# Attention layers of a graph network on one core: engines held to program order, row-half transposes, reciprocals through memory

## The chip, the core and the metric

The kernel runs on one core of a Trainium2 chip. The core has a matrix engine (TensorE, PE in the profile; its weight loads are the row PEld), a vector engine (VectorE, DVE), a scalar engine (ScalarE, ACT), a general one (GpSimd, POOL) and a queue for transfers (SyncE, SP). Each of them takes its own instructions one after the other, and semaphores tie the engines together. The matrix engine writes to PSUM, a memory of eight banks, from which DVE and ACT read. The metric is the device time of one execution in microseconds; less is better.

## The reference, cut to what matters

```python
# x: (32, 512, 64), adj: (512, 512); all float32
h = relu(layernorm(x)); x = x + graph_layer_0(h, adj)
h = relu(layernorm(x)); x = x + graph_layer_1(h, adj)

# layer 2: one attention head
h = relu(layernorm(x))
Wh = h @ W.T
e = leaky_relu((Wh @ a1)[:, :, None] + (Wh @ a2)[:, None, :], 0.2)
att = softmax(where(adj > 0, e, -9e15), axis=-1)
x = x + elu(att @ Wh)

# layer 3: eight heads of width 128, then one more attention over their outputs
h = relu(layernorm(x))
def gat_layer(x, W, b):
    g = x @ W
    s = einsum('bnd,bmd->bnm', g, g) * adj
    s = where(s == 0, -1e16, s)
    return softmax(s, axis=2) @ g + b
cat = leaky_relu(concat over the 8 heads of gat_layer(h, Wh[i], bh[i]), 0.01)
x = x + leaky_relu(gat_layer(cat, W_out, b_out), 0.01)
```

## The kernel before

Layers 0 and 1 come first and take the first 265 us or so; they are not touched. Layers 2 and 3 are one stream of *units*. A unit holds two attention matrices of 512 x 512: two graphs of the batch in layer 2 (`Gat`, 16 units), two heads of one graph in layer 3 (`Heads`, 128 units), or the last attention of two graphs (`Out`, 16 units). The order of units is written out: the 16 `Gat`, then the `Heads` of one graph after the other (four units each), with an `Out` put in after the third unit of the graph that follows its pair; so eight `Heads` and one `Out` repeat, and the last `Out` comes after three empty places.

A unit takes four steps in each of its phases, one for each block of 128 rows or columns (`C` = 4). The function `run` walks over steps `k` and lets the units that are in flight do one step of each phase. In step `r` of the unit whose scores are computed, the following happens:

- `scores(r)`: PE multiplies (L547, tile `s_ps`, two banks, two buffers). In `Gat` there is nothing to do here.
- `transpose(j)` of the unit before, with an offset of five steps (`C + LAG`): the exponentials `p_att` are turned, eight transposes of 128 x 128 into two banks `pt_ps` (L413), which ACT copies into `pt_att` (L418). With `j == 1`, `recips` follows: DVE takes the reciprocals of the row sums (L432), PE spreads them over partitions with 16 matmuls against the identity (L436, tile `rec_ps`), and ACT copies the result to `recb` (L444).
- `values(j)`, offset six: PE multiplies `pt_att` with the values into `av` (L425), one bank with one buffer.
- `end(step)`, offset ten: step 0 multiplies `av` by `recb` on DVE (`normalize`, L448); step 1 of `Heads` multiplies with the head's weights (L619, `y_ps`, two products) and lets ACT make `cat` of it (L624); step 2 of `Gat` and `Out` adds the result to `x` (`back`).
- `prep(step)` of the unit to come, four steps ahead: `Heads` normalizes its graph at step 0 when it is the graph's first unit (`hn`, `hx`), and makes `g` at step 2 (L591, copied by ACT at L599). `Out` multiplies `cat` with `W_out` into `gT_ps` (L642), four products in each of its four steps, then makes `gT` and `gV`.
- `soft(r)`: DVE multiplies the scores with the adjacency (L536), finds the zeros (L540), and adds and takes the row minimum for each of the two matrices (L397); ACT takes the exponentials and their sums (L401).

What a matmul of float32 is in the source stands as two in the profile; a transpose is one.

The pool `ps_m` has three banks under one tag. `pt_ps`, `rec_ps`, `y_ps`, `g_ps`, `gT_ps`, `hx_ps`, `back_ps` and the small products of `Gat` take turns in them. `ps_s` has the four banks of the scores, `ps_v` the one of `av`.

The order in which instructions stand on each engine is not that of the source: a planner of the tile framework sets it from dependencies, priorities and its own costs. In layer 3 it puts, on PE, a block of transposes, a block of values and a block of scores in turn, and fits the other products between them; on DVE it lets `normalize`, the reciprocals and the work on `hn` slip in between the four operations of a soft step.

Of the kernel before, what the change touches and what calls it, by code (L numbers as in the profile page):

```python
# [8 lines left out]
F32 = mybir.dt.float32  # L9
# [5 lines left out]
P = 128  # L15
# [7 lines left out]
def gnn_stack_kernel(  # L23
# [22 lines left out]
    nc = tc.nc  # L46
    B, N, F = x.shape
    C = N // P
    H, _, D = w_heads.shape
# [4 lines left out]
    const = ctx.enter_context(tc.tile_pool(name="const", bufs=1))  # L54
    xpool = ctx.enter_context(tc.tile_pool(name="xpool", bufs=1))
    tiny = ctx.enter_context(tc.tile_pool(name="tiny", bufs=4))

    ident = const.tile([P, P], F32, name="ident")
# [10 lines left out]
    for g in range(NG):  # L69
        xg = xpool.tile([P, G, C, F], F32, name=f"x{g}")  # L70
        step = 2 if g == 0 else G
# [37 lines left out]
    wo_sb = const.tile([P, H, F], F32, name="wo_sb")  # L109
# [224 lines left out]
        return wk.tile([P, N], F32, name=name, tag="row", bufs=2 * H + 6)  # L334

    wk = ctx.enter_context(tc.tile_pool(name="work_b", bufs=2))
    ps_s = ctx.enter_context(tc.tile_pool(name="ps_s", bufs=2, space=PSUM))
    ps_m = ctx.enter_context(tc.tile_pool(name="ps_m", bufs=3, space=PSUM))
    ps_v = ctx.enter_context(tc.tile_pool(name="ps_v", bufs=1, space=PSUM))
# [1 line left out]
    adj_f = adj_p.rearrange("p c k q -> p c (k q)")  # L341
    neg = const.tile([P, C, N], F32, name="neg")
    nc.vector.tensor_scalar(neg, adj_f, 0.0, GAT_NEG, op0=OP.is_le, op1=OP.mult)

# [30 lines left out]
    def halves(k):  # L377
        return slice(k * F, (k + 1) * F)

    class Pair:  # L380
# [26 lines left out]
        def transpose(self, j):  # L407
            pt = pbuf.tile([P, 2, N], F32, name="pt_att", bufs=3)
            self.pts = getattr(self, "pts", []) + [pt]
            for k in range(2):  # L410
                ps = ps_m.tile([P, N], F32, name="pt_ps", tag="m")
                for r in range(C):
                    nc.tensor.transpose(  # L413
                        ps[:, r * P : (r + 1) * P],
                        self.p[:, k, r, j * P : (j + 1) * P],
                        ident,
                    )
                nc.scalar.copy(pt[:, k, :], ps)  # L418

        def values(self, j):  # L420
            pt = self.pts.pop(0)
# [6 lines left out]
                )  # L428

        def recips(self):  # L430
            rec = tiny.tile([P, 2, C], F32, name="rec")
            nc.vector.reciprocal(rec, self.sum)  # L432
            ps = ps_m.tile([P, N], F32, name="rec_ps", tag="m")
            for r in range(C):
                for k in range(2):
                    nc.tensor.matmul(  # L436
                        ps[halves(k), r * P : (r + 1) * P],
                        lhsT=rec[:, k, r : r + 1].to_broadcast([P, F]),
                        rhs=ident,
                        start=True,  # L440
                        stop=True,
                    )
            self.recb = wk.tile([P, N], F32, name="recb")
            nc.scalar.copy(self.recb, ps)  # L444

        def normalize(self):
            self.o = wk.tile([P, N], F32, name="o_att")
# [107 lines left out]
    class Heads(Pair):  # L555
# [9 lines left out]
        def prep(self, step):  # L565
            b, i = self.b, self.i
            if step == 0 and i == 0:
# [9 lines left out]
                    h[:, :, 0, :], h[:, :, 0, :], 0.0,  # L577
                    rstd[:, cols, None].to_broadcast([P, C, F]), op0=OP.max, op1=OP.mult,
                )
                nc.vector.tensor_copy(h[:, :, 1, :], h[:, :, 0, :])  # L580
                Heads.hn[b] = h
                Heads.hx[b] = pair_transpose(
                    ps_m, lambda n: wk.tile([P, N], F32, name=n), h, "hx",
                    nc.vector.tensor_copy, "m",
                )
            elif step == 2:
                rows = halves(i % 2)
# [41 lines left out]
    class Out(Pair):  # L629


        def __init__(self, b):
            self.b = b

        def prep(self, step):
            b = self.b
            if step == 0:
                self.gps = ps_m.tile([P, N], F32, name="gT_ps", tag="m")
            if step < 4:
                for h in (2 * step, 2 * step + 1):  # L640
                    for k in range(2):
                        nc.tensor.matmul(  # L642
                            self.gps[halves(k), :], lhsT=wo_sb[:, h, :],
                            rhs=Heads.cat[b + k, h], start=(h == 0), stop=(h == H - 1),
                        )
            if step == 3:
                self.gT = wk.tile([P, N], F32, name="gT")
                nc.scalar.copy(self.gT, self.gps)
                ps = ps_m.tile([P, C, P], F32, name="gV_ps", tag="m")
                for c in range(C):  # L650
                    nc.tensor.transpose(ps[:, c], self.gT[:, c * P : (c + 1) * P], ident)
                self.gV = wk.tile([P, C, P], F32, name="gV")
                nc.scalar.copy(self.gV, ps)
# [30 lines left out]
    def run(units):  # L684
        units = units + [None] * 3

        def at(k, off):
            u, j = divmod(k - off, C)
            return (units[u], j) if 0 <= u < len(units) else (None, j)

        for j in range(C):
            units[0].prep(j)
        for k in range(len(units) * C):
            cur, r = at(k, 0)
            if cur:
                cur.scores(r)
            u, j = at(k, C + LAG)
            if u:
                u.transpose(j)
                if j == 1:  # L700
                    u.recips()
            u, j = at(k, C + LAG + 1)
            if u:
                u.values(j)
            u, j = at(k, 2 * C + LAG + 1)
            if u:
                u.end(j)
            u, j = at(k, -C)
            if u:
                u.prep(j)  # L710
            if cur:
                cur.soft(r)

    flow_stats = []
    order = [Gat(b) for b in range(0, B, 2)]
# [45 lines left out]
```

## Time and profile before

| | us |
|---|---|
| median of 3 runs | 2914.0 (2912.58 to 2915.0) |
| the profiled execution, its own time | 2918.14 |
| its span, first to last instruction | 2916.4 |
| PE busy | 2813.4 |
| PEld busy | 1380.0 |
| DVE busy | 2407.5 |
| ACT busy | 2049.0 |
| POOL busy | 52.7 |

The mean TensorE clock that was granted is 0.983 of the full one. The profile comes from one execution, and times of single instructions are taken from it. A row of the timeline gives the start and the length in us, the engine, the line, the operation, the output and input tiles and their sizes; in brackets stands how long the engine was idle before it, and which engine, tile and line ended that. Matmuls are pipelined and their ends are modelled, so the distance between starts tells what one costs.

### The profile page before, as it was taken

The page shows a single profiled execution, that of the slowest core. Times are in us where ns is not written, and L with a number is a line of the kernel's source. Part 1 is how long each engine was busy: PE and PEld are TensorE (multiplying, and loading weights), DVE is VectorE, ACT ScalarE, POOL GpSimd, SP SyncE. Part 2 cuts the span into 40 slices and gives each one's busy share as a digit, 9 for nine tenths or more (in the row PEclk, how much of TensorE's full clock was granted, in tenths as well). Part 3 has the DMA queues.
Part 4 walks back from the last instruction along what each step waited for, and adds up shares of the span by engine and source line. Part 5 has one row for each costly group of instructions (what it writes and reads, how often), then busy time and mean ns, then how long its engine had stood idle before and what let it go on. Part 6 is the DMA issues. An engine that isn't in the chain of part 4 may idle for free.

```text
span 2916.4 us, 41809 instructions
## 1 busy us (share of the span) xinstructions
PE 2813.4 (96%) x15532; PEld 1380.0 (47%) x15532; DVE 2407.5 (83%) x4870; ACT 2049.0 (70%) x4687; POOL 52.7 (2%) x49
## 2 busy tenths in 40 slices
PE   7998887899999999999999999999999999999998
PEld 4555544444444444444444444444444444444443
DVE  6665889899798988888888888888888888888884
ACT  2333767677777778777777777777777777777775
POOL 3000000000000000000000000000000000000000
PEclk9998999899999999999999999999999999999999
DMA  3000000000000000000000000000000000000000
GB/s 86 1 1 1 1 1 1 1 1 1 1 5 4 1 4 1 4 1 5 1 4 1 4 1 4 1 5 1 4 1 5 1 5 1 4 1 4 1 4 4
DMA packets 9916, 13.10 MB, mean 4 GB/s; under 512 B 1016, under 2 KB 9376, under 8 KB 9584
## 3 DMA queue, kind: packets, MB, share of 16 engines
q1 hardware_dynamic: 4752, 5.24, 0.5%
q10 hardware_dynamic: 4208, 4.19, 0.5%
q8 instruction: 122, 2.00, 0.3%
q0 software_dynamic: 752, 0.99, 0.2%
q14 instruction: 82, 0.67, 0.1%
HBM read 6.23 MB, written 4.19 MB: 4 GB/s over the span
## 4 chain that ended last, share of the span: by engine, by line
PE 88%; DVE 6%; ACT 3%; issue 1%; POOL 1%; DMA 1%; POOLq 0%; DVEq 0%; ACTq 0%
PE av L425 20%; PE pt_ps L413 20%; PE s_ps L547 19%; PE rec_ps L436 6%; PE g_ps L591 5%; PE y_ps L619 4%; PE nt_ps L240 4%; PE gT_ps L642 3%; PE nt1b_ps L240 2%; ACT p_att L401 1%; DVE s_att L536 1%; PE po L251 1%; DVE t_att L397 1%; PE wh_ps L474 1%; DVE l_att L397 1%
## 5 line engine op out<-in xcount | busy, mean ns | idle before, releaser
L401 ACT ACTIVATE p_att<-t_att,negmax 128x512 f32<-128x512 f32 x1152 | 825.3, 717 | 466.3 <-DVE negmax L397 466.2
L536 DVE TENSOR_TENSOR s_att<-s_ps,adj_p 128x1024 f32<-128x1024 f32 x576 | 703.3, 1221 | 228.6 <-PE s_ps L547 228.6
L413 PEld LDWEIGHTS pt_ps<-ident,p_att 128*128 128x128 f32 x5120 | 554.8, 142 | 492.6 <-ACT p_att L401 187.5
L418 ACT COPY pt_att<-pt_ps 128x512 f32<-128x512 f32 x1280 | 679.3, 581 | 120.7 <-PE pt_ps L413 120.5
L397 DVE CUSTOM_DVE_ANT_0 t_att<-s_att,t_att 128x512 f32<-128x512 f32 x1152 | 752.3, 687 | 13.4
L413 PE MATMUL pt_ps<-ident,p_att 128*128 128x128 f32 x5120 | 714.5, 282 | 12.6 <-ACT p_att L401 7.5
L547 PE MATMUL s_ps<-hx,g 64*128 64x512 f32 x2048 | 661.2, 625 | 2.0 <-DVE s_att L536 2.0
L425 PE MATMUL av<-pt_att,hn 128*64 128x512 f32 x2048 | 579.0, 611 | 0.0
L540 DVE TENSOR_SCALAR t_att<-s_att 128x1024 f32<-128x1024 f32 x576 | 393.1, 683 | 24.3 <-ACT pt_att L418 0.5
L547 PEld LDWEIGHTS s_ps<-hx,g 64*128 64x128 f32 x2048 | 204.8, 185 | 311.3 <-issue 121.3
L401 ACT ACTIVATION_READ_ACCUMULATOR p_att<-t_att,negmax 128x1 f32 x1152 | 216.0, 187 | 0.0
L436 PE MATMUL rec_ps<-ident,rec 128*64 128x128 f32 x2560 | 186.6, 284 | 16.9 <-DVE rec L432 10.6
L436 PEld LDWEIGHTS rec_ps<-ident,rec 128*64 128x64 f32 x2560 | 144.4, 139 | 50.6 <-issue 26.5
L624 ACT ACTIVATE cat<-y_ps,bh 128x512 f32<-128x512 f32 x256 | 159.6, 672 | 4.4 <-PE y_ps L619 4.4
L425 PEld LDWEIGHTS av<-pt_att,hn 128*64 128x64 f32 x2048 | 115.6, 135 | 76.5 <-issue 76.2
L619 PE MATMUL y_ps<-o_att,wh_sb 64*128 64x512 f32 x512 | 145.8, 641 | 1.6 <-ACT pt_att L418 0.8
L591 PE MATMUL g_ps<-hx,m 64*128 64x512 f32 x256 | 144.6, 645 | 1.0 <-ACT pt_att L418 0.9
L642 PE MATMUL gT_ps<-cat,wo_sb 128*64 128x512 f32 x512 | 131.4, 595 | 0.0
L448 DVE TENSOR_TENSOR o_att<-av,recb 128x512 f32<-128x512 f32 x160 | 108.9, 681 | 21.8 <-PE av L425 20.6
L240 PE MATMUL nt_ps<-adj_t,hn 128*128 128x512 f32 x256 | 116.5, 598 | 0.0
L397 DVE DVE_READ_ACCUMULATOR2_ANT negmax<- 128x1 f32 x1280 | 104.7, 82 | 0.0
L444 ACT COPY recb<-rec_ps 128x512 f32<-128x512 f32 x160 | 93.9, 587 | 8.8 <-PE rec_ps L436 8.8
(131 smaller groups left out, 1930.4 us busy)
## 6 DMA issues: line engine op xcount, KB each, us to landing
out_dram<-x SPq DMA_DIRECT2D x32, 128.0 KB, 1.8
x<-in_x_dram ACTq DMA_DIRECT2D x3, 1024.0 KB, 13.7
x<-in_x_dram ACTq DMA_DIRECT2D x4, 256.0 KB, 7.9
adj_raw<-in_adj_dram SPq DMA_DIRECT2D x1, 1024.0 KB, 5.3
wh_sb<-in_L_gnn_Wh_dram POOLq DMA_DIRECT2D x2, 256.0 KB, 8.0
wo_sb<-in_L_gnn_W_out_dram POOLq DMA_DIRECT2D x1, 256.0 KB, 7.9
wl<-in_L_gnn_net_params_dram POOLq DMA_DIRECT2D x4, 16.0 KB, 7.0
bias_b<-in_L_gnn_bias_dram POOLq DMA_DIRECT2D x1, 32.0 KB, 7.6
```

Source lines behind the costliest of these rows:

```text
L240: nc.tensor.matmul(p, lhsT=lhs(k), rhs=adj_t[:, k, :], start=(k == 0), stop=(k == C - 1))
L397: nc.vector.tensor_tensor_reduce(out=ns[k], in0=s[k], in1=t[k], scale=-1.0, scalar=BIG, op0=OP.add, op1=OP.min, accum_out=self.negmax[:, k ...
L401: nc.scalar.activation(self.p[:, k, r, :], ns[k], AF.Exp, bias=self.negmax[:, k, r : r + 1], scale=-1.0, accum_out=self.sum[:, k, r : r + 1],)
L413: nc.tensor.transpose(ps[:, r * P : (r + 1) * P], self.p[:, k, r, j * P : (j + 1) * P], ident,)
L418: nc.scalar.copy(pt[:, k, :], ps)
L425: nc.tensor.matmul(self.av[halves(k), :], lhsT=self.v(k, j), rhs=pt[:, k, :], start=(j == 0), stop=(j == C - 1),)
L436: nc.tensor.matmul(ps[halves(k), r * P : (r + 1) * P], lhsT=rec[:, k, r : r + 1].to_broadcast([P, F]), rhs=ident, start=True, stop=True,)
L536: nc.vector.tensor_tensor(s, ps, adj_f[:, r, None, :].to_broadcast([P, 2, N]), OP.mult)
L540: nc.vector.tensor_scalar(t, s, 0.0, FLOW_NEG, op0=OP.is_equal, op1=OP.mult)
L547: nc.tensor.matmul(u.s_ps[:, k], lhsT=g[halves(k), r * P : (r + 1) * P], rhs=x[halves(k), :], start=True, stop=True,)
L591: nc.tensor.matmul(ps, lhsT=m2[rows, 2 * i : 2 * i + 2, :].rearrange("p h f -> p (h f)"), rhs=self.x[rows, :], start=True, stop=True,)
L619: nc.tensor.matmul(ps, lhsT=wh_sb[halves(k), h, :], rhs=self.o[halves(k), :], start=True, stop=True,)
```

## The change

The part of `run` with all units is put under `tc.manual_schedule` for PE, DVE and ACT: on these three engines the instructions stand in the order in which the source emits them. The source order itself is changed: `end` now comes before `values`, `soft` comes before `recips` and `prep`, and `recips` moves from `j == 1` to `j == 0` of the transposes.

The transposes of a step are made on row halves: 16 of 64 x 128 in place of eight of 128 x 128, the halves of the rows in a bank each, and ACT copies each bank to interleaved places of `pt_att`.

The reciprocals no longer go through PE and ACT. DVE writes them into one of two zeroed tiles of 128 x 32, turns that tile in blocks of 32 x 32, SP writes the rows to a buffer in DRAM with four transfers, and two further transfers read them back, spread over 64 partitions each, into `recb`.

The product with `W_out` is spread: `Out.prep` is also called four and eight steps earlier, and puts one head's products in a step, from step -7 to step 1; `gT` is copied at step 1, `gV` made at step 2. Two copies of `Heads.prep` (for `hn` and `hx`) go from DVE to ACT.

```diff
+    dram = ctx.enter_context(
+        tc.tile_pool(name="dram", bufs=3, space=bass.MemoryType.DRAM)
+    )
...
+    recs = [const.tile([P, 32], F32, name=f"rec{i}") for i in range(2)]
+    for rec in recs:
+        nc.gpsimd.memset(rec, 0.0)
...
         def transpose(self, j):
             pt = pbuf.tile([P, 2, N], F32, name="pt_att", bufs=3)
             self.pts = getattr(self, "pts", []) + [pt]
+            ps = [ps_m.tile([P, 2, C, F], F32, name="pt_ps", tag="m") for half in range(2)]
             for k in range(2):
-                ps = ps_m.tile([P, N], F32, name="pt_ps", tag="m")
                 for r in range(C):
-                    nc.tensor.transpose(
-                        ps[:, r * P : (r + 1) * P],
-                        self.p[:, k, r, j * P : (j + 1) * P],
-                        ident,
-                    )
-                nc.scalar.copy(pt[:, k, :], ps)
+                    for half in range(2):
+                        nc.tensor.transpose(
+                            ps[half][:, k, r],
+                            self.p[halves(half), k, r, j * P : (j + 1) * P],
+                            ident[halves(half), halves(half)],
+                        )
+            pth = pt.rearrange("p k (r half q) -> p k r half q", r=C, half=2)
+            for half in range(2):
+                nc.scalar.copy(pth[:, :, :, half, :], ps[half])
...
         def recips(self):
-            rec = tiny.tile([P, 2, C], F32, name="rec")
-            nc.vector.reciprocal(rec, self.sum)
-            ps = ps_m.tile([P, N], F32, name="rec_ps", tag="m")
-            for r in range(C):
-                for k in range(2):
-                    nc.tensor.matmul(
-                        ps[halves(k), r * P : (r + 1) * P],
-                        lhsT=rec[:, k, r : r + 1].to_broadcast([P, F]),
-                        rhs=ident,
-                        start=True,
-                        stop=True,
-                    )
+            rec = recs[0]
+            recs.append(recs.pop(0))
+            nc.vector.reciprocal(rec[:, : 2 * C], self.sum.rearrange("p k r -> p (k r)"))
+            rect = tiny.tile([P, 32], F32, name="rect")
+            nc.vector.transpose(rect, rec)
+            row = dram.tile([2 * C, P], F32, name="rec_row")
+            for q in range(P // 32):
+                nc.sync.dma_start(
+                    row[:, q * 32 : (q + 1) * 32], rect[q * 32 : q * 32 + 2 * C, :]
+                )
             self.recb = wk.tile([P, N], F32, name="recb")
-            nc.scalar.copy(self.recb, ps)
+            for k in range(2):
+                nc.sync.dma_start(
+                    self.recb[halves(k), :],
+                    row[k * C : (k + 1) * C]
+                    .rearrange("(o r) p -> o (r p)", o=1)
+                    .to_broadcast([F, N]),
+                )
...
         # Heads.prep, step 0
-                nc.vector.tensor_copy(h[:, :, 1, :], h[:, :, 0, :])
+                nc.scalar.copy(h[:, :, 1, :], h[:, :, 0, :])
...
-                    nc.vector.tensor_copy, "m",
+                    nc.scalar.copy, "m",
...
         # Out.prep
-            if step == 0:
+            if step == -2 * C + 1:
                 self.gps = ps_m.tile([P, N], F32, name="gT_ps", tag="m")
-            if step < 4:
-                for h in (2 * step, 2 * step + 1):
-                    for k in range(2):
-                        nc.tensor.matmul(
-                            self.gps[halves(k), :], lhsT=wo_sb[:, h, :],
-                            rhs=Heads.cat[b + k, h], start=(h == 0), stop=(h == H - 1),
-                        )
-            if step == 3:
-                self.gT = wk.tile([P, N], F32, name="gT")
-                nc.scalar.copy(self.gT, self.gps)
+            h = H - 2 + step if step >= 0 else 2 * C - 1 + step
+            if 0 <= h < (H if step >= 0 else H - 2):
+                for k in range(2):
+                    nc.tensor.matmul(
+                        self.gps[halves(k), :], lhsT=wo_sb[:, h, :],
+                        rhs=Heads.cat[b + k, h], start=(h == 0), stop=(h == H - 1),
+                    )
+                if h == H - 1:
+                    self.gT = wk.tile([P, N], F32, name="gT")
+                    nc.scalar.copy(self.gT, self.gps)
+            if step == 2:
                 ps = ps_m.tile([P, C, P], F32, name="gV_ps", tag="m")
...
-        for k in range(len(units) * C):
+        with tc.manual_schedule(engines={PE, DVE, Activation}):
+            for j in range(C):
+                units[0].prep(j)
+            for k in range(len(units) * C):
                 cur, r = at(k, 0)
                 if cur:
                     cur.scores(r)
                 u, j = at(k, C + LAG)
                 if u:
                     u.transpose(j)
-                    if j == 1:
-                        u.recips()
+                u, j = at(k, 2 * C + LAG + 1)
+                if u:
+                    u.end(j)
                 u, j = at(k, C + LAG + 1)
                 if u:
                     u.values(j)
-                u, j = at(k, 2 * C + LAG + 1)
-                if u:
-                    u.end(j)
-                u, j = at(k, -C)
-                if u:
-                    u.prep(j)
                 if cur:
                     cur.soft(r)
+                u, j = at(k, C + LAG)
+                if u and j == 0:
+                    u.recips()
+                for early in range(2, -1, -1):
+                    u, j = at(k, -C * (early + 1))
+                    if u and (early == 0 or isinstance(u, Out)):
+                        u.prep(j - early * C)
```

The rows of the profile before name the lines of the kernel before. In the changed kernel the transposes stand at L422 and their copies at L429, values at L436, the reciprocal at L446, normalize at L465, scores at L564, the soft step at L553, L557, L404 and L408, g at L608, y at L636, W_out at L661.

## The prediction

> **What bounds the kernel now.** I read the page first, then stretches, then one stretch of the timeline, and last the waits. The page says that PE is busy nearly all the time and at full clock:
>
> ```profile
> PE 2813.4 (96%) x15532; PEld 1380.0 (47%) x15532; DVE 2407.5 (83%) x4870; ACT 2049.0 (70%) x4687; POOL 52.7 (2%) x49
> ...
> PE   7998887899999999999999999999999999999998
> PEclk9998999899999999999999999999999999999999
> ```
>
> The table of stretches for the layer-3 part (640 to 2800 us; columns: length, then busy time of PE, PEld, DVE, ACT, POOL, then clock) shows PE busy 2156.6 of 2160 us, DVE 1844.8:
>
> ```profile
> 640.00:2800.00 2160.00, 2156.58 (x12217) 1009.94 (x12217) 1844.83 (x3636) 1633.85 (x3775) 0.00 (x0) 1.00 0.01 3
> ```
>
> In it stand 2156 matmuls of L547, 16 to a unit (4 steps): 134.75 units, **16.03 us a unit**. In the list of waits for that stretch DVE waits for PE:
>
> ```profile
> DVE s_att L536 <- PE s_ps L547: 211.8, 257, 3.1
> ```
>
> One stretch of the timeline (start, length, both us) gives the spacings that I use:
>
> ```profile
> 1512.33 1.22 DVE L536 TENSOR_TENSOR s_att<-s_ps,adj_p 128x1024 f32<-128x1024 f32 x1
> ...
> 1513.58 0.69 DVE L540 TENSOR_SCALAR t_att<-s_att 128x1024 f32<-128x1024 f32 x1
> ...
> 1514.31 0.69 DVE L397 CUSTOM_DVE_ANT_0 t_att<-s_att,t_att 128x512 f32<-128x512 f32 x1
> ...
> 1514.93 0.69 DVE L397 CUSTOM_DVE_ANT_0 t_att<-s_att,t_att 128x512 f32<-128x512 f32 x1
> 1515.05 0.72 ACT L401 ACTIVATE p_att<-t_att,negmax 128x512 f32<-128x512 f32 x1 [0.25 <-DVE negmax L397]
> ...
> 1515.77 0.71 ACT L401 ACTIVATE p_att<-t_att,negmax 128x512 f32<-128x512 f32 x1
> ...
> 1515.95 1.09 PE L413 MATMUL pt_ps<-ident,p_att 128*128 128x128 f32 x8
> ...
> 1516.47 0.56 ACT L599 COPY g<-g_ps 128x512 f32<-128x512 f32 x1
> 1516.94 1.07 ACT L418 COPY pt_att<-pt_ps 128x512 f32<-128x512 f32 x2
> ...
> 1516.98 1.08 PE L425 MATMUL av<-pt_att,hn 128*64 128x512 f32 x4
> ...
> 1517.99 1.13 PE L547 MATMUL s_ps<-hx,g 64*128 64x512 f32 x4
> ```
>
> A PE step is three blocks, 1.03, 1.01 and about 1.05 us from start to start: some 0.86 of work and 0.17 lost at each change of array shape. A DVE step in program order is 1.25 + 0.73 + 0.62 + 0.62 = **3.22 us**.
>
> **What the Trainium skill says.** "TensorEngine Tiling (Array Packing)", Key Properties: changing the tiling mode drains TensorE; the 0.17 us agrees. Its Gotcha 1: row tiles need different PSUM banks, hence two banks for each transpose. "PSUM — Partial Sum Buffer", Engine vs sequencer instructions: the ScalarE and VectorE queues are strict FIFO and matmuls start in program order, so an instruction that waits holds all behind it; the trace of before shows no case against it. "TensorE: Matmul & The Clock Gate", Part 1: PE falls to half clock after an idle window of about 3.4 us. Here less is enough: a 1.42 us gap was followed by about 3.3 us at 0.5:
>
> ```profile
> 315.82 1.78 PE L436 MATMUL rec_ps<-ident,rec 128*64 128x128 f32 x16 [1.42 <-ACT p_att L401]
> ...
> 317.00:318.00 1.00, 1.00 (x8) 0.50 0.00 0
> ```
>
> **The change, part by part.** Steps are r0 to r3 of a unit; t2 is the start of DVE's L536 (L553 after) in r2.
>
> *Half transposes.* The nearest row is a transpose of 64 rows:
>
> ```profile
> 262.49 0.68 PE L354 MATMUL whT_ps<-ident,wh_sb 64*128 64x64 f32 x8 [0.89 <-PE po1b L251]
> ```
>
> With 0.22 of latency taken off, its 8 start every 0.066 us. Sixteen halves cost 0.5 us a step if the two row groups run together, 1.05 if not; I take 0.5. Scores and transposes now have one shape, so one drain of three goes. *Reciprocals:* 16 matmuls, 0.9 us a unit, leave PE, and a 0.59 us copy leaves ACT. DVE gains a 32x32 transpose, not in the trace: 0.15 us (0.1 to 0.5; the reciprocal beside it takes 0.20). On SP come 4 writes and 2 broadcast reads of 128 KB a unit; the only 128 KB store shown lands in 1.8 us, so two dependent hops are some 5 us (4 to 10) against five steps (over 16 us) until L465 (normalize) needs them: hidden, and an output store queued behind them has no reader. If the cover failed, normalize would be late by the excess. POOL's two memsets lie ahead of layer 2.
>
> PE per unit becomes 4 x (0.86 + 0.5 + 0.17 + 0.86 + 0.17) = 10.2, plus y 0.86, g 0.86, W_out 0.76, the rest 0.35: **13.1 us**. DVE alone needs 4 x 3.22 + 0.61 (normalize) + 0.35 = **13.84**. PE stops being the bound; without new waits a unit would lose 2.2 us. But the order is now fixed, and I follow what is late next.
>
> *y behind ACT.* With end ahead of values, y's products stand in front of values on PE. ps_m has three banks. In r3 the transposes take two; g_ps of r2 holds the third. y's first product waits for the g copy, its second for the first pt_att copy of the same step; on ACT both stand behind the exponentials of r2. From t2: second L404 at 2.60, exps at 2.72 and 3.44, g copy 4.14, pt copy 4.61 to 5.18, y's second product 5.28 to 6.13, drain, values at 6.30, scores at 7.31, ready 8.44, so L553 of the next r0 at 8.5. DVE would be there at 6.44: **2.06 us lost**, in each unit with a y. Such a unit takes 15.9 us, what it took before.
>
> *W_out spread.* gT_ps now holds one of the three banks for nine steps of every nine units, over two of these r2-r3 edges. There the transposes also wait for the g copy (4.80), the copies end at 6.1 and 6.6, y at 7.55, values and one W_out product bring scores to 9.6: DVE at 10.8, 2.3 us more.
>
> *hx.* Twice in nine units, in r0, PE's queue holds the hx transposes between values and the next scores. Its two copies now stand on ACT (DVE is rid of 0.29 and 0.69 us, ACT gets about as much). The transposes wait for the ACT copy of hn, which waits for DVE's two hn steps after the whole soft step: ready 4.6 us after the step began, scores at 5.3, DVE at 6.4, not 3.22: 3.2 us each, 0.85 of it DVE's own. *back_ps* of an Out in front of r0 costs 1.9, and the unit in which Out would have its y saves 2.06.
>
> Nine units: 6 x 15.9 + 2 x 18.2 + 13.84 + 2 x 3.2 + 1.9 = 153.9 us, before 9 x 16.03 = 144.2. The order has 16 such nines: **+155 us**.
>
> *Layer 2* is near DVE's limit already (253.9 busy of 300 us from 250 to 550; one unit from 433.7 to 449.75). In program order DVE stops at ht's transposes (0.8), at lo behind two pt copies and its exponential (1.65), at e2s behind the exponentials of the step (1.6): about 4.2 us on 16 units, **+67** (30 to 100), and the statistics now stand open before POOL's squares (2.3 us each, 1.8 shown at most): **+10**. The end saves most of the 7.09 us block of L642: **-6**.
>
> *Clock.* In r2 values wait for normalize (one ps_v bank), so PE stands about 2.3 us, with only transposes before. I take half of these gaps to be followed by half clock, delaying y by 1.2 us: 0.6 x 128 units = **+80**; the bounds are 0, if only a whole empty window counts, and 350, if PE stays slow for half the time.
>
> Sum: 155 + 67 + 10 - 6 + 80 = +306 on the profiled execution's own 2918.1 us (span 2916.4): 3224. The median of the runs shown is 4 us lower: **3220**.
>
> **Rivals.** *A, faster, 0.07:* y's bank is free in time. The chain above is my reading of the queues; if y's products cost no wait, nine units take 153.9 - 8 x 2.06 - 2 x 2.3 = 132.8, which is -182, and with +71 for the rest about 2805. It decides when y's loss, edges included, falls under 0.9 us a unit (then the nine take 139.8, -71, and the +71 is just made up). For it: DVE idles 15% now and PE is relieved. Against it: the order of ACT's queue is fixed. *B, slower still, 0.12:* PE's clock stays low. Half-clock for half of the time makes 13.1 into 19.7 us a unit: 144 x 3.7 + 77 = about 3520. For it: in layer 2 the clock was 0.87 with PE busy 81%. *C, 0.01: no change:* the 15.9 us units stand, while hx, gT_ps, layer 2 and clock cost nothing, 2905 to 2920. *D, the halves do not pair:* this is inside the forecast, since PE has room; only the gT_ps edges see it, 32 x 0.5 = +16.
>
> **Numbers.** The forecast has 0.80. Its low end has no clock loss (3140), half of layer 2's loss and 0.4 us less in each y chain: 3140 - 34 - 51 = 3055, so 3050; the high end reaches into B: 3500. That leaves out A, C and the rest of B. Slower than +0.2% (about what a measurement of this kernel can tell from no change): 0.92; within 0.2%: 0.01; faster: 0.07.
>
> **What would show it.** PE's busy share near 75%, DVE's below before. In the waits: L553 behind scores about 2 us in r0; PE at y behind the pt_att copy; PE at values behind normalize; hx transposes behind the hn copy; no wait on recb; PEclk below 9 in many slices. A layer-3 unit of 14 us, or L553 never waiting over 1 us, would make the prediction wrong.

## The result, and the profile after

The changed kernel takes **3286.6 us** (median of 4 runs, 3282.3 to 3293.6); the kernel before, run beside it, 2914.4 (2912.6 to 2915.0). The ratio is 1.128, with a 95% interval of 1.126 to 1.130: slower by some 372 us. The forecast was 3220 us (3050 to 3500). The profiled execution has a span of 3283.1 us against 2916.4.

Layer 3 begins with the first scores on PE. In the trace of before they start at 568.7 us, in that of after at 667.7: **99.0 us** of the 366.7 us between the two spans lie ahead of layer 3, and 267.7 in it.

The page of after, the same rows as shown of before:

```profile
PE 2630.1 (80%) x18092; PEld 1199.5 (37%) x18092; DVE 2453.5 (75%) x4966; ACT 2017.0 (61%) x4591; POOL 50.0 (2%) x51
...
PE   7996655568888888888888888888888888888887
...
PEclk9997777788999999999999999998999999999998
```

No engine is busy all the time now. PE fell from 96% to 80% and VectorE from 83% to 75%; the clock row is lowest in slices 4 to 8 (0.7), which is layer 2. The chain that ended last shows two engines taking turns, where before PE alone had 88% of it:

```profile
DVE 39%; PE 38%; ACT 10%; issue 4%; POOL 0%; DVEq 0%; POOLq 0%; ACTq 0%
```

The table of stretches for 700 to 2700 us (length, busy time of PE, PEld, DVE, ACT, POOL, then clock), and from the list of waits for that stretch (us in total, times, longest) the one of VectorE for scores and those of PE that the prediction named:

```profile
700.00:2700.00 2000.00, 1651.15 (x11868) 705.38 (x11866) 1557.19 (x3077) 1330.61 (x3058) 3.78 (x2) 0.93 0.05 17
```

```profile
DVE s_att L553 <- PE s_ps L564: 367.5, 183, 6.4
...
PE av L436 <- DVE o_att L465: 156.8, 109, 2.2
...
PE hx_ps L178 <- ACT hn L597: 80.2, 25, 3.2
...
PE y_ps L636 <- ACT g L616: 38.5, 37, 1.0
...
PE y_ps L636 <- ACT pt_att L429: 16.2, 24, 0.7
```

All the waits that the prediction named are there, PE at y behind the pt_att copy in its last row and more often behind the g copy, and none on recb is. To see which step pays, I took every start of VectorE's L553 from 700 to 2428 us in the timeline, with the wait for scores printed beside it, and named the steps r0 to r3 by the reciprocals, which follow r1 (97 units or so; 144 in the kernel). A wait stands under the step that it holds up. The kernels of the experiments are in the table too:

| kernel | first scores | unit | ahead of r0 | r1 | r2 | r3 | clock, 700 to 2700 |
|---|---|---|---|---|---|---|---|
| before | 568.7 | 16.04 | | | | | 1.00 |
| after | 667.7 | 17.87 | 1.92 | 0.78 | 0.00 | 0.69 | 0.93 |
| e3: y late, g early | 674.7 | 16.16 | 0.39 | 0.79 | 0.06 | 0.30 | 0.95 |
| e4: normalize early | 643.9 | 18.35 | 3.17 | 0.76 | 0.00 | 0.03 | 0.90 |
| e5: hn early | 669.9 | 16.75 | 1.70 | 0.02 | 0.00 | 0.58 | 0.96 |
| e6: all three | 664.1 | 15.13 | 0.33 | 0.05 | 0.00 | 0.43 | 0.99 |
| e8: full transposes | 655.6 | 17.39 | 1.64 | 0.84 | 0.02 | 0.35 | 0.97 |
| e9: halves twice | 679.8 | 17.88 | 1.99 | 0.86 | 0.00 | 0.33 | 0.97 |
| e10: W_out in 3 steps | 672.0 | 17.86 | 1.53 | 1.01 | 0.00 | 0.72 | 0.93 |
| e12: e6, W_out, layer 2 | 581.4 | 14.99 | 0.43 | 0.30 | 0.00 | 0.00 | 1.00 |

A unit of after takes 17.87 us, of which VectorE waits 3.39 for scores; 144 x (17.87 - 16.04) is 264 us, nearly the whole loss of layer 3. (In before the order moves between units, so its waits aren't split by step.)

One unit of the timeline (start, length, and in brackets the wait and who ended it):

```profile
1712.89 0.66 DVE L465 TENSOR_TENSOR o_att<-av,recb 128x512 f32<-128x512 f32 x1
...
1713.47 1.21 DVE L553 TENSOR_TENSOR s_att<-s_ps,adj_p 128x1024 f32<-128x1024 f32 x1
...
1713.70 1.08 PE L436 MATMUL av<-pt_att,gV 128*64 128x512 f32 x4 [1.46 <-DVE o_att L465]
...
1717.61 0.56 ACT L616 COPY g<-g_ps 128x512 f32<-128x512 f32 x1
1718.07 0.69 DVE L557 TENSOR_SCALAR t_att<-s_att 128x1024 f32<-128x1024 f32 x1
1718.07 1.07 ACT L429 COPY pt_att<-pt_ps 128x512 f32<-128x512 f32 x2
...
1718.22 1.61 PE L636 MATMUL y_ps<-o_att,wh_sb 64*128 64x512 f32 x4 [1.05 <-ACT g L616]
...
1719.76 1.08 PE L436 MATMUL av<-pt_att,gV 128*64 128x512 f32 x4
...
1720.77 1.13 PE L564 MATMUL s_ps<-hx,g 64*128 64x512 f32 x4
...
1721.95 1.22 DVE L553 TENSOR_TENSOR s_att<-s_ps,adj_p 128x1024 f32<-128x1024 f32 x1 [1.84 <-PE s_ps L564]
```

The row at 1713.47 is the start of r2. What follows is the y chain link by link: y stands until the g copy, which stands behind r2's exponentials; y's second product ends behind the first pt_att copy; then values, then scores, then VectorE, which has stood 1.84 us.

### The profile page after: what moved, and what is told of

Read it like the earlier page. It is cut to its first block, busy times and chain, and to the rows that moved or that the text cites. A ratio compares the mean times of both kernels' runs of the same rounds, so it can differ in the third digit from the quotient of the medians.

```text
span 3283.1 us, 48830 instructions
## 1 busy us (share of the span) xinstructions
PE 2630.1 (80%) x18092; PEld 1199.5 (37%) x18092; DVE 2453.5 (75%) x4966; ACT 2017.0 (61%) x4591; POOL 50.0 (2%) x51
## 4 chain that ended last, share of the span: by engine, by line
DVE 39%; PE 38%; ACT 10%; issue 4%; POOL 0%; DVEq 0%; POOLq 0%; ACTq 0%
DVE s_att L553 12%; DVE t_att L404 11%; PE av L436 10%; PE s_ps L564 9%; DVE t_att L557 7%; PE y_ps L636 7%; ACT p_att L408 6%; PE pt_ps L422 5%; DVE o_att L465 3%; PE g_ps L608 3%; PE gT_ps L661 1%; DVE l_att L524 1%; ACT pt_att L429 1%; ACT g L616 1%; DVE l_att L404 1%
## 5 line engine op out<-in xcount | busy, mean ns | idle before, releaser
L408 ACT ACTIVATE p_att<-t_att,negmax 128x512 f32<-128x512 f32 x1152 | 821.0, 715 | 555.2 <-DVE negmax L404 555.2
L553 DVE TENSOR_TENSOR s_att<-s_ps,adj_p 128x1024 f32<-128x1024 f32 x576 | 702.9, 1220 | 477.7 <-PE s_ps L564 468.2
L429 ACT COPY pt_att<-pt_ps 128x512 f32<-128x512 f32 x1280 | 680.1, 582 | 294.8 <-PE pt_ps L422 294.6
L564 PE MATMUL s_ps<-hx,g 64*128 64x512 f32 x2048 | 764.1, 701 | 15.6 <-DVE s_att L553 10.6
L404 DVE CUSTOM_DVE_ANT_0 t_att<-s_att,t_att 128x512 f32<-128x512 f32 x1152 | 751.1, 689 | 19.6
L436 PE MATMUL av<-pt_att,hn 128*64 128x512 f32 x2048 | 598.3, 663 | 189.1 <-DVE o_att L465 189.1
L422 PEld LDWEIGHTS pt_ps<-ident,p_att 64*128 64x128 f32 x10240 | 499.5, 149 | 491.3 <-issue 273.6
L422 PE MATMUL pt_ps<-ident,p_att 64*128 64x64 f32 x10240 | 541.0, 235 | 101.3 <-ACT e L516 56.5
L557 DVE TENSOR_SCALAR t_att<-s_att 128x1024 f32<-128x1024 f32 x576 | 399.5, 694 | 51.3 <-ACT pt_att L429 0.9
L564 PEld LDWEIGHTS s_ps<-hx,g 64*128 64x128 f32 x2048 | 223.4, 204 | 410.8 <-issue 161.8
L636 PE MATMUL y_ps<-o_att,wh_sb 64*128 64x512 f32 x512 | 229.8, 661 | 89.8 <-ACT g L616 47.9
L436 PEld LDWEIGHTS av<-pt_att,hn 128*64 128x64 f32 x2048 | 108.0, 140 | 318.3 <-ACT p_att L408 163.5
L408 ACT ACTIVATION_READ_ACCUMULATOR p_att<-t_att,negmax 128x1 f32 x1152 | 216.6, 188 | 0.0
L608 PE MATMUL g_ps<-hx,m 64*128 64x512 f32 x256 | 184.6, 809 | 0.0
L408 ACT ACTIVATE p_att<-l_att,negmax 128x512 f32<-128x512 f32 x128 | 91.3, 714 | 89.7 <-DVE negmax L404 89.5
L661 PE MATMUL gT_ps<-cat,wo_sb 128*64 128x512 f32 x512 | 133.9, 600 | 0.0
L636 PEld LDWEIGHTS y_ps<-o_att,wh_sb 64*128 64x128 f32 x512 | 76.3, 187 | 145.4 <-ACT pt_att L429 67.4
L465 DVE TENSOR_TENSOR o_att<-av,recb 128x512 f32<-128x512 f32 x160 | 106.8, 667 | 23.4 <-PE av L436 23.1
L178 PE MATMUL hx_ps<-ident,hn 128*128 128x128 f32 x128 | 27.6, 352 | 103.0 <-ACT hn L597 103.0
L178 PE MATMUL ht_ps<-ident,hn 128*128 128x128 f32 x128 | 27.5, 355 | 101.4 <-DVE hn L169 101.1
```

The costliest lines, as they stand in the source:

```text
L404: nc.vector.tensor_tensor_reduce(out=ns[k], in0=s[k], in1=t[k], scale=-1.0, scalar=BIG, op0=OP.add, op1=OP.min, accum_out=self.negmax[:, k ...
L408: nc.scalar.activation(self.p[:, k, r, :], ns[k], AF.Exp, bias=self.negmax[:, k, r : r + 1], scale=-1.0, accum_out=self.sum[:, k, r : r + 1],)
L422: nc.tensor.transpose(ps[half][:, k, r], self.p[halves(half), k, r, j * P : (j + 1) * P], ident[halves(half), halves(half)],)
L429: nc.scalar.copy(pth[:, :, :, half, :], ps[half])
L436: nc.tensor.matmul(self.av[halves(k), :], lhsT=self.v(k, j), rhs=pt[:, k, :], start=(j == 0), stop=(j == C - 1),)
L465: nc.vector.tensor_tensor(self.o, self.av, self.recb, OP.mult)
```

## The experiments

Each experiment ran beside the kernel before on one chip, 4 runs or more of each; the medians of the kernel before were 2916.8 to 2918.6 us there. The changed kernel was not run again, so a difference from it is one of medians (3286.6 us), and a few us of it mean nothing. The edits are shortened.

**The order and the parts, crossed.** e2 is the kernel before with the fixed order alone; e1 is the changed kernel without it.

```diff
 e2 (on the kernel before)                   e1 (on the changed kernel)
+with tc.manual_schedule(engines={PE,        -with tc.manual_schedule(engines={PE,
+        DVE, Activation}):                  -        DVE, Activation}):
     for j in range(C): ...                       for j in range(C): ...
```

> The kernel before with only the fixed program order (PE, DVE, ScalarE) put around its own loop; nothing else of the change. Theory (the order is what costs): slower than 2914 by over 150 us, 3050 to 3400 us, with both layers slower. Rival (a fixed order is harmless where transposes, reciprocals and W_out are as before): 2880 to 2950 us.

> The fixed order alone is undone: half transposes, DMA reciprocals, the ScalarE copies and the spread W_out stay, the planner orders the engines again. Theory (the order is what costs): PE has 13.1 us of work a layer-3 unit and DVE 13.84, so a unit falls below the 16.03 us of the kernel before; 14.5 to 15.5 us, total 2700 to 2850 us, layer 3 starts near 570 us, clock 0.95 or more. Rival (a part other than the order costs: halves that lower the clock, reciprocals by DMA, gT_ps holding its bank): 2914 us or more.

| | planner's order | fixed order |
|---|---|---|
| parts as before | 2914.4 | e2: 3201.3 (ratio 1.098, 1.096 to 1.099) |
| parts as changed | e1: 2995.4 (ratio 1.028, 1.025 to 1.031) | 3286.6 |

Fixing the order costs 287 us with the old parts and 291 with the new ones, so the order is the main cost, as expected. The two fixed orders are not the same one, though, and the near agreement of the two numbers is no more than that: e2 fixes the old loop's order, in which y stands behind values. Its layer 2 is slower still, with first scores at 697.4 us, and its unit of 17.1 us has other waits (from 700 to 2700 us VectorE stands 53.9 us for hx_ps and 31.2 for back_ps). e1 keeps the changed order of the source, from which the planner starts. But e1 contradicts the rest of my expectation: with the planner's order the new parts are **slower** than the old ones by 81 us, though PE's work did shrink (1839.8 us busy of 2000 against 1996.9). Some 15 us of the 81 lie ahead of layer 3 (first scores at 584.1 us); its unit takes 16.48 us. The list of waits of e1, 700 to 2700 us, says why:

```profile
DVE rec L446 <- ACT p_att L408: 204.9, 108, 4.5
```

The planner puts the reciprocals right behind the last exponential that feeds them, ahead of the next L553 in VectorE's queue, and VectorE stands there 1.9 us each time, 108 times in some 121 units. In the kernel before the same wait comes to 61.5 us in all. There `recips` came a step later in the program; the change moved it to `j == 0`, which is harmless only where the program's order holds (there it comes behind r1's work, and no such wait shows). That the 81 us are this wait is read from the trace and wasn't tried by itself.

**Layer 2 alone.** e7 enters the fixed order with the first layer-3 unit:

```diff
+        steps(range(n2))                    # n2 = C * (B // 2), planner's order
+        with tc.manual_schedule(engines={PE, DVE, Activation}):
+            steps(range(n2, len(units) * C))
```

> The fixed order is entered only from the first layer-3 unit on; layer 2 is ordered by the planner, all else as in the changed kernel. Theory (layer 2 pays 99 us for its fixed order: first scores at 667.7 against 568.7 us): first scores near 570 us, total near 3190 us (3170 to 3210). Rival (layer 2 is slower by the half transposes and the DMA reciprocals, or by its low clock whatever the order): first scores after 640 us, total 3255 us or more.

3199.7 us (3195.1 to 3214.0), first scores at 576.2 us, and the unit of layer 3 stays what it was (17.95 us). Of the 99 us, 91.5 come back by the order alone; 7.5 are left to the other parts, a remainder that moves with the planner's order (e11 below starts layer 3 at 572.7 us, e1 at 584.1). In the changed kernel's list of VectorE's waits from 300 to 520 us the longest rows are:

```profile
DVE e L506 <- PE e_ps L499: 14.0, 9, 1.9
DVE e2s L517 <- ACT e L516: 13.0, 9, 1.4
DVE x L473 <- PE back_ps L471: 12.9, 8, 1.7
DVE ht L180 <- PE ht_ps L178: 11.4, 9, 1.3
DVE lo L540 <- ACT lo L539: 11.0, 8, 1.4
```

The first row is mostly not new: in the kernel before it is 13.6 us in 12 stops over the same 220 us. The other four, of 1.44, 1.61, 1.27 and 1.38 us a stop, hardly stand there (4.9 us together). From 272 us to the first scores of layer 3 VectorE is idle for 126.6 us in the trace of after and for 35.7 in that of before: 91 us more, of which these four rows make 74, e 6 and the statistics 5.

**The y chain.** e3 moves two things that hold y: its products go behind values, and g is made in r1, so its copy and its bank are out of r3's way. The two were not tried apart.

```diff
-                if u: u.end(j)
-                ...
-                if u: u.values(j)
+                if u and j == 0: u.end(j)        # normalize stays ahead
+                ...
+                if u: u.values(j)
+                ...
+                if u and j > 0: u.end(j)
...
-            elif step == 2:                      # Heads.prep: g
+            elif step == 1:
```

> In the fixed order, the products y are issued behind the values of the same step instead of ahead of them, and g is made one step earlier (r1), so that its bank and its copy are out of the way; all else as in the changed kernel. Theory (y behind ScalarE's queue costs about 2 us in each of 128 units, 2.3 more at 32 W_out edges): 225 to 300 us less, total 2990 to 3060 us, DVE's wait for scores at r0 falls under 1 us. Rival (the low clock and the hx wait hold the step, y's place does not matter): 3230 us or more.

3041.9 us (3038.8 to 3044.8): 245 us less, inside the theory's range. The wait ahead of r0 falls from 1.92 to 0.39 us; this alone is 144 x 1.53 = 220 us. y's place, together with g's, is the largest cause in layer 3.

**hx.** e5 computes and copies hn one step before its transposes (`prep` is called early for `Heads` too):

```diff
-            if step == 0 and i == 0:             # hn, and hx at once
+            if step == -1 and i == 0:            # hn
...
+            elif step == 0 and i == 0:           # hx
```

> In the fixed order, hn of the next batch element is computed (VectorE) and copied (ScalarE) one step ahead of its hx transposes, so that TensorE's queue no longer waits for the copy. All else as in the changed kernel. Theory (the hx wait costs 2.3 us, 32 times): 3195 to 3230 us, TensorE's wait of 3.2 us at hx gone. Rival (the wait lies in slack that another wait fills): 3265 to 3300 us.

3136.7 us (3130.4 to 3143.0): 150 us less, **twice** what I expected. The wait ahead of r1 is all but gone (0.78 to 0.02, 109 us in 144 units), and those ahead of r0 and r3 shrank by 0.22 and 0.11. In after, VectorE stood ahead of r1 in 25 of 95 units, 2.96 us each where I had 2.35. The timeline of after shows the difference: PE stands 3.21 us ahead of hx in all 22 cases from 700 to 2428 us, and in 21 of them the scores behind hx then take 1.48 to 2.08 us instead of 1.13:

```profile
1613.28 0.66 PE L178 MATMUL hx_ps<-ident,hn 128*128 128x128 f32 x4 [3.21 <-ACT hn L597]
1613.86 2.08 PE L564 MATMUL s_ps<-hx,g 64*128 64x512 f32 x4
```

**Normalize.** e4 takes away the gap of PE ahead of values in r2. `end(0)` leaves its old place, in layer 2 too, and goes into the soft step of r1:

```diff
         t = wk.tile([P, 2, N], F32, name="t_att", bufs=3)
         nc.vector.tensor_scalar(t, s, ...)
+        if first: first.end(0)                   # normalize of the unit before, in r1
         s, t = ...
```

> In the fixed order, normalize is issued one step earlier: on VectorE in r1, between t_att and the row maxima, instead of behind the whole step r1 and the reciprocals. Values of r2 then find it done and TensorE has no gap there. All else as in the changed kernel. Theory (the gap of some 2 us in r2 costs by the half clock that follows, about 0.6 to 0.9 us a unit): 3160 to 3220 us, granted clock in layer 3 from 0.93 to 0.97 or more, the half-clock stretches gone. Rival (the clock is low beside the path, only the y chain counts): 3265 to 3300 us.

3342.2 us (3324.8 to 3351.8): **slower by 56 us**, against both expectations. Step by step the table shows what happened: the wait ahead of r3 is gone (0.69 to 0.03), as the theory had it, but the one ahead of r0 rose from 1.92 to 3.17. (Layer 2 gained from the move, with first scores at 643.9 us in place of 667.7, so that layer 3 alone lost some 80 us.) PE now has its work for r2 done early and stands in r3 instead, in front of y. From the list of waits of e4 for 700 to 2700 us, then its timeline, then PE's table of stretches (length, busy time of PE, clock):

```profile
PE y_ps L640 <- ACT g L620: 135.9, 62, 2.4
```

```profile
1533.62 2.24 PE L640 MATMUL y_ps<-o_att,wh_sb 64*128 64x512 f32 x4 [2.35 <-ACT g L620]
...
1539.82 1.23 DVE L555 TENSOR_TENSOR s_att<-s_ps,adj_p 128x1024 f32<-128x1024 f32 x1 [4.38 <-PE s_ps L568]
```

```profile
1535.00:1536.00 1.00, 1.00 (x4) 0.50 0.00 0
```

The gap was moved, not removed: PE has less work than VectorE either way. In after it lay ahead of values; in e4 it lies ahead of y, and y, values and scores, all on the chain, run at 0.50. The stretch from the start of r2 to that of the next r0 shows what this costs. In units with a y and without a W_out product it takes 8.48 us in after and 8.44 in e4 where the clock stays full; with half clock in it, it takes 9.4 us in after (28 of 65 such units) and 10.5 in e4 (38 of 63).

**W_out.** e10 puts its products into three steps:

```diff
-            if step == -2 * C + 1: self.gps = ...
-            h = H - 2 + step if step >= 0 else 2 * C - 1 + step
+            if step == -1: self.gps = ...
+            for h in {-1: (0, 1), 0: (2, 3, 4, 5), 1: (6, 7)}.get(step, ()):
```

> W_out's products are put into three steps (r3 after its values, r0, r1) in place of nine, so that gT_ps no longer holds a bank over an r2-r3 edge; all else as in the changed kernel. Theory (the held bank costs 2.3 us on 32 edges): 74 us less, 3190 to 3230 us; the VectorE waits of 3.5 us and more at r0 gone. Rival (those waits are y's own and stay): 3265 us or more.

3282.6 us (3279.3 to 3286.2), ratio to before 1.125 (1.123 to 1.127): **no difference** that can be told from the changed kernel, as the rival's time has it, but not by its reason. The long waits did go: ahead of r0, 20 of 95 were 3.25 us or more in after, 4 of 95 here, and the mean fell by 0.39 us, or 56 us in 144 units. What came in their place is in the timeline:

```profile
1507.29 3.60 PE L660 MATMUL gT_ps<-cat,wo_sb 128*64 128x512 f32 x16
```

Four heads in one step take 3.60 us of PE ahead of the scores for r1, and the wait there rose by 0.23 us a unit, 33 us in all; 4 us more lie ahead of r3 and 4 ahead of layer 3, and some 10 us stay without an account. The held bank costs about what was predicted; this cure costs nearly as much.

**The halves and the clock.** e8 undoes the halves, e9 repeats them:

```diff
 e8                                            e9
-  ps = [ps_m.tile([P, 2, C, F]) x 2 halves]    -  for k in range(2):
+  for k in range(2):                           +  for k in [0, 1, 0, 1]:
+      ps = ps_m.tile([P, N])                      for r in range(C):
       for r in range(C): transpose 128x128            for half in range(2): ...
+      nc.scalar.copy(pt[:, k, :], ps)
```

> The transposes of p_att are full 128x128 again, 8 a step, one bank for each k; fixed order and the rest as in the changed kernel. Theory (TensorE is not the bound, and y waits for ScalarE's queue either way): 0 to 0.5 us more a unit, 3285 to 3370 us. Rival (the halves themselves, 16 small products and their weight loads, are what made the kernel slower): under 3230 us.

> Every half transpose is issued twice into the same place (32 a step for 16): useless work on TensorE, 0.5 us a step more, nothing else of the changed kernel altered. Theory (the halves leave TensorE so idle that its clock falls, and the half clock costs more than they save; this is why full transposes were 79 us faster): faster than the changed kernel, 3190 to 3260 us, clock in layer 3 at least 0.96 against 0.93. Rival (full transposes were faster by their copies, one bank ready after half the work, and not by the clock): 3287 us or more.

e8 takes 3207.8 us (3201.8 to 3211.9): 79 us **less** than with halves. e9 takes 3282.1 us (3279.0 to 3284.9), ratio 1.125 (1.123 to 1.127): no difference. Neither theory was right. Both kernels raise the clock of layer 3 from 0.93 to 0.97 and take the same 0.34 to 0.36 us off the wait ahead of r3, some 50 us in 144 units. So giving PE more to do does bring the clock back, and by these waits it is worth about 50 us; no run gained that by the clock alone. In e9 the longer steps take it back (0.07 more ahead of r0, 0.08 ahead of r1, and back_ps later), and layer 3 starts 12 us later. In e8 it starts 12 us earlier. There the wait ahead of r0 also falls, by 0.28, and the waits of 3.25 us or more there are gone altogether (20 of 95 in after, 10 of 95 in e9). That fits the banks: a half transpose needs both banks before either copy may begin, a full one fills bank after bank, so that an edge with gT_ps stops less. This was not tried by itself.

**Together.** e6 is e3, e4 and e5 in one kernel; e11 is e6 with layer 2 under the planner as in e7; e12 is e11 with e10's W_out.

> The three moves together in the fixed order: y behind values with g a step earlier, normalize a step earlier, hn a step ahead of hx. Theory (these three hold the layer-3 unit above VectorE's own 13.84 us): 14.3 to 14.9 us a unit, total 2770 to 2880 us, faster than the kernel before although layer 2 still pays 99 us. Rival (another wait, such as gT_ps's bank or ScalarE's queue, takes their place): 15.6 us a unit or more, 2960 us or more.

> The three moves (y behind values with g a step earlier, normalize a step earlier, hn ahead of hx) with layer 2 left to the planner. Theory (layer 2's loss and layer 3's add up): 2907 less 90, 2800 to 2835 us, first layer-3 scores near 576 us. Rival (the entry from one order into the other costs what layer 2 gains): 2880 us or more.

> The same with W_out's products in three steps (r3, r0, r1) in place of nine. Theory (of VectorE's waits left in the three moves, 0.43 us a unit ahead of r3 and some of 0.33 ahead of r0 are gT_ps's bank): 45 to 75 us under the kernel of the three moves with layer 2 planned, 2740 to 2780 us. Rival (six products in two steps make TensorE late there): no more than 20 us gained.

e6: 2907.3 us (2904.8 to 2908.8, 9 runs), ratio 0.997 (0.996 to 0.998): 379 us under the changed kernel, more than the 245 + 150 - 56 of the single edits. Normalize a step earlier, a loss by itself, is none once y no longer waits: the clock is 0.99. The unit of 15.13 us is neither the theory's (14.3 to 14.9) nor the rival's (15.6): 0.43 us are left ahead of r3. e11: 2817.3 us (2814.0 to 2822.1), ratio 0.966 (0.964 to 0.968); layer 2's gain adds whole (90 us). e12: **2794.4 us** (2787.8 to 2796.5), ratio **0.957 (0.955 to 0.959)**: 23 us more, between the two theories. The wait ahead of r3 is gone; in 13 of some 115 units there is one of 2.3 us ahead of r0, in 13 one of 2.6 us ahead of r1, each with W_out's products in front of it on PE.

The list of waits of e12 for 700 to 2700 us, to set beside that of after (367.5, 183, 6.4):

```profile
DVE s_att L555 <- PE s_ps L568: 95.2, 103, 2.6
```

So a kernel with the half transposes and the reciprocals by DMA can be faster than the one before; it was the order fixed around them that cost. Whether the old parts would do as well in this last order was not tried, nor were the reciprocals by DMA or the two copies on ScalarE undone by themselves in the fixed order.

## Why the prediction held, point by point

The direction and the mechanism were right; the size was 67 us short, 2% of the time and 18% of the loss. Of the 61 us that the two spans show, 39 are in layer 3 (229 predicted with its clock and its end, 267.7 measured) and 22 in layer 2 with the statistics (77 and 99). The unit of layer 3, cut at the starts of r0 and r2 (L553), against the prediction's own terms (us; measured from 700 to 2428 us, with the number of units):

| stretch | predicted | measured |
|---|---|---|
| r2 to the next r0, with y, full clock | 8.5 | 8.48 (37) |
| the same at an edge with W_out's bank held | 10.8 | 10.43 (12) |
| the same without y, back_ps in it | 6.44 + 1.9 = 8.34 | 7.60 (2) |
| added by half clock in this stretch, mean of all units | 80 / 144 = 0.55 | about 0.6 |
| r0 to r2 without hx | 2 x 3.22 + 0.61 + 0.35 = 7.40 | 7.60 (64; 7.51 in 10 more) |
| the same with hx | 7.40 + 3.2 = 10.6 | 11.67 (21) |
| mean unit | 17.65 | 17.87 |

- **VectorE's step of 3.22 us**: too small. It was read from a step whose second operation starts 1.25 us after the first. In after this distance is 1.33 us in r0, r1 and r3, with a wait or without, and 1.25 only in r2, where L553 follows normalize (1709.23 to 1710.56 in an r1, 1713.47 to 1714.72 in the r2 behind it). From r0 to r2 the units take 0.20 us more than the sum, which is 29 us in 144 units. From r2 to r0 the longer step costs nothing where y's chain sets the end: VectorE only comes to its wait later.
- **Half transposes pair**: right. Sixteen take 0.66 us with their latency, where 8 full ones take 1.09 (e8). Rival D is out:

```profile
1709.01 0.66 PE L422 MATMUL pt_ps<-ident,p_att 64*128 64x64 f32 x16
```

  But "PE has room" was too kind to them: full transposes were 79 us faster in this order, by the clock and, as far as read, by the banks. The prediction had put nothing against the halves beyond the common clock term.
- **Reciprocals hidden**: right. VectorE's transpose takes 0.21 us (0.15 taken). In the timeline the four writes start at 1712.99 us and the two reads at 1715.22; no wait on recb shows anywhere.
- **y behind ACT, 2.06 us**: right link by link. Counted from 1713.47 in the unit shown above, the g copy starts at 4.14 us (4.14 predicted), the pt_att copies at 4.60 (4.61), values at 6.29 (6.30), scores at 7.30 (7.31) and the next L553 at 8.48 (8.5). VectorE waits 1.84 us and not 2.06 because it comes 0.2 us later. Waits of 1.75 to 2.25 us are the commonest ahead of r0 (37 of 95); the mean of 1.92 also holds 24 waits of 1 us, behind waits of some 1.6 us ahead of r3: the two share one chain. e3 shortens the stretch from 8.48 to 6.77 us and gave back 245 us.
- **W_out's bank, 2.3 us at two edges of nine units**: right in number (20 of 95 waits of 3.25 us and more; e10 leaves 4) and a little large: 10.43 - 8.48 = 1.95 us where the clock was full. Of this 0.74 us stands ahead of r3, where one of W_out's products lies between values and scores.
- **hx, 2.35 us net of VectorE's own 0.85**: right in kind, too small. The stretch is 1.07 us longer than the sum, and VectorE waits 2.96 us; the step "scores at 5.3, DVE at 6.4" took full clock behind a gap of 3.2 us. This gap was not in the clock term, which counted the one in r2 alone. With the 0.20 us of the steps taken off, it is 0.87 us, 28 us for 32 such units.
- **back_ps, 1.9 us**: what can be read is less, 0.8 us more of step r3 in 11 of 95 units.
- **Clock, +80 (0 to 350)**: the right size, and in part by luck, since neither the half of the gaps nor the 1.2 us for each was read from a trace. Half clock stood between r2 and the next r0 in 44 of 95 units. A unit with y then took 9.4 us there in place of 8.48, one without y 9.09 in place of 7.60, and those at W_out's edges some 2 us more. As the difference from units of the same kind at full clock this is about 0.6 us a unit in the mean, some 80 us. The waits ahead of r3 agree: 32 of 1.60 us, all with half clock, 20 of 0.74 at the edges of W_out at full clock, and none in the other 43. The gap in r2 is there too (PE at values behind normalize): of 40 gaps of 2 us and more from 700 to 2428 us, 22 were followed by values at half clock.
- **Layer 2, +67**: ht, lo and e2s were put at 0.8, 1.65 and 1.6 us and measured 1.27, 1.38 and 1.44. The missing term is VectorE's stop for back_ps, 20.1 us in 13 stops over the layer against 1.2 before, which I had looked for in layer 3 alone. It is nearly all of the 22 us.
- **Rival A** needed y's loss under 0.9 us a unit. In the changed kernel it is twice that, and even where it is made so small (e3, 0.39 us) the unit is 16.16 us and not A's 132.8 / 9 = 14.76, since VectorE's own work is longer and the gaps of PE ahead of hx and values still cost. **Rival B** did not come: the clock in layer 3 was 0.93. **Rival C** is out with the same waits.
- **The signs**: the waits came as listed; two shares did not. PE was busy 80% and not near 75%, and the clock row is below 9 in nine slices of 40 only, five of them in layer 2.

## What to carry to other kernels

When a change makes one engine's work less, ask who is late next under the order that now holds: here PE's busy time fell by 183 us and the kernel's time rose by 372, because an instruction in PE's fixed queue waited for a copy at the end of ScalarE's. Follow each instruction with a cross-engine wait through its queue, and count its bank, its place and the gap it leaves; three such moves, of one step or less, were worth 379 us together. An edit that moves a gap must be priced at the place where the gap ends up.

## What was not expected of the hardware

PE's clock does not go by the length of a gap alone, and the loss falls on whatever comes next. "TensorE: Matmul & The Clock Gate" of the Trainium skill (Part 1) speaks of an idle window of about 3.4 us; here the window need not be idle. In e4 a gap of 2.35 us was followed by 0.50, and in after 21 of 22 gaps of 3.21 us by slow scores, but one of them not. The traces show more. In each of them the clock changes only on a fixed raster of 3.41 us, so that a stretch at half clock lasts one, two or more such windows. I took PE's busy share (with its modelled ends) in each window at full clock, from 700 to 2700 us. In after, all 60 windows with less than 45% were followed by a window at half clock, none of the 349 with 70% or more were, and 14 of the 90 between. In the 14 traces together it is 375 of 376 and 4 of 6439. So it matters how a gap falls on the raster: one of 2.2 us within a window leaves PE busy for at most 36% of it, and the same gap shared by two windows can leave both above half. That fits gaps of one length with both outcomes. Useless work on PE brought the clock from 0.93 to 0.97 at no cost in time. And products on 64 rows of the array run beside each other when they follow in the queue: at 1714.70 us the first g product and at 1714.72 the first scores began, two products of one row half each.
